# Causal masking of the score maxima: added on TensorE, or inside VectorE's maximum

## The chip, the core and the metric

The kernel runs on one core of one Trainium2 chip. The metric is device time in microseconds (us) from start to end of one launch. Engines are called as in the profile: PE is TensorE's matmul stream and PEld its weight loads, DVE is VectorE, ACT is ScalarE, POOL is GpSimd, SP issues DMAs.

## The reference

Input `x` is 4 batches of 1024 tokens of 256 channels. First, x becomes x + layernorm(g * s), where s is a tanh recurrence over the 1024 tokens of the layer-normed input and g a sigmoid gate. Then x becomes x + layernorm(block(layernorm(x))), where the block is causal attention followed by a top-2-of-4 mixture of experts. The attention, which is what the change touches:

```python
q = _rms(heads(wq), qn_w); k = _rms(heads(wk), kn_w); v = heads(wv)   # 16 heads of 16
scores = jnp.einsum('bhqd,bhkd->bhqk', q, k) * HD ** (-0.5)
scores = jnp.where(causal[None, None], scores, -jnp.inf)
attn = jax.nn.softmax(scores, axis=-1)
```

## The kernel before

The 1024 tokens are cut into 8 chunks of 128 (`NI`); a tile of the attention is one chunk of queries of one batch, 32 tiles in all. For each chunk there are projections for the recurrence, the recurrence itself (one POOL add at L554 and one ACT tanh at L557 per token), layer norms, and projections to q, k, v. A tile of chunk i meets the i+1 key chunks up to its own, for 16 heads: four head groups `hc`, each with four heads on partitions 0, 32, 64 and 96. A block is one pair (hc, key chunk): 128 queries by 128 keys for each of its four heads.

Scores are made twice. "s" has queries on partitions and serves only to find each query's maximum over its keys; the negated maximum is then written into a spare slot of the query vector (`pad[:, 0, :, HD]`), the query is transposed again (`q2`), and "sT" (keys on partitions) comes out of the product with the maximum already taken off. ACT takes the exponential of sT (L979), POOL sets its non-causal entries to zero (L999), and the products with the values are summed in `av` (L1016). A maximum that is too large is harmless for the result of a softmax, as it only rescales numerator and sum.

The blocks of a tile are cut into steps of at most four blocks (`cuts`; chunk 6 alternates four and three). One step for one pair of heads fills two PSUM banks, one per head, up to 512 columns each. `scores()` interleaves the sT products of an earlier tile with the s products of a later one, so that a turn of it takes four of the seven `bank` tiles. Where a step holds a block on the diagonal (key chunk equal to query chunk), the s part ends at L898: a bf16 product of the identity (`ident_h`) with `mask` (0 on and below the diagonal, -3e38 above) adds the mask onto the diagonal blocks of each bank. `look_maxima()` then has DVE reduce each bank with a negated maximum (L937), in one instruction for each run of blocks of one head group, or one for a bank that holds two or four equal runs.

A helper, `Plan`, decides the order in which instructions of all engines are written, from costs given with each `Op` and from which bank or slot would be free first; on the chip each engine runs its own list in that order and waits on semaphores. [...] Banks go back to the plan after the exponential (sT) or after the maximum (s). After the attention come the experts (L1435 to L1574), gathered by token lists.

Of the kernel before, what the change touches and what calls it, by code (L numbers as in the profile page):

```python
# [11 lines left out]
BF16 = mybir.dt.bfloat16  # L12
AF = mybir.ActivationFunctionType
ALU = mybir.AluOpType
# [4 lines left out]
P = 128  # L19
# [18 lines left out]
FMAX = 3.4028234663852886e38  # L38
# [207 lines left out]
def sandwich(  # L246
# [7 lines left out]
    nc = tc.nc  # L254
    ctx.enter_context(tc.manual_schedule())
    wp = ctx.enter_context(tc.tile_pool(name="wp", bufs=1))
# [6 lines left out]
    banks = Banks([psum.tile([P, 512], F32, name=f"bank{n}") for n in range(7)])  # L263
# [30 lines left out]


    ident_h = wp.tile([P, P], BF16, name="ident_h")
    mask = wp.tile([P, P], BF16, name="mask")

    low = wp.tile([P, E, E], F32, name="low")
    nlow = wp.tile([P, E, E], F32, name="nlow")  # L300
# [19 lines left out]
    def once():  # L320

        yield Op("SP", 2.0, 50.0, [ev("x", 0)], lag=8.0)
        for t, ap in loads:
            nc.sync.dma_start(t, ap)
        done("loaded")
        yield Op("DVE", 2.0, 50.0, [ev("st", 0)])
        nc.vector.tensor_copy(ident_h, ident)
        nc.vector.memset(av, 0.0)
        nc.vector.memset(qn_s, 1.0)
        for s in range(4):  # L330
            sl = slice(32 * s, 32 * s + HD)
            nc.vector.tensor_scalar_mul(qn_s[sl], qn_w[sl], HD ** -0.5)

        nc.vector.memset(listed, 0.0)

        nothing = sqs.tiles[0].rearrange("p h d -> p (h d)")[:, :C]
        nc.vector.memset(nothing, 0.0)
        some = nothing.unsqueeze(1)
        for c0, c1 in ((0, C), (2 * C, ROW)):
            nc.sync.dma_start(  # L340
                of_chunk(NI - 1, c0, c1), some[:, :, : c1 - c0].to_broadcast([P, B, c1 - c0])
            )
        for k in range(11):
            nc.sync.dma_start(
                row_d[TOKENS : TOKENS + 1, k * ROW // 11 : (k + 1) * ROW // 11],
                nothing[0:1, : ROW // 11],
            )
        for p in pads.tiles:
            yield Op("DVE", 1.2, 50.0)


            nc.vector.memset(p, 0.0)
            nc.vector.memset(p[:, 1, :, HD : HD + 1], 1.0)
        for cc in range(NCC):
            yield Op("DVE", 1.1, 50.0, [ev("loaded")])
            nc.vector.tensor_scalar_mul(wqk[:, cc, :], wqk[:, cc, :], n1_w[:, cc : cc + 1])
            nc.vector.tensor_scalar_mul(wv[:, cc, :], wv[:, cc, :], n1_w[:, cc : cc + 1])
            nc.vector.tensor_scalar_mul(wg[:, cc, :], wg[:, cc, :], n2_w[:, cc : cc + 1])
        for h in range(0, H, 4):
            yield Op("DVE", 1.2, 50.0)  # L360
            for b in range(B):
                nc.vector.memset(v_all[:, b, :, h : h + 4, HD : HD + 1], 1.0)
        nc.vector.memset(low, 0.0)
        nc.vector.memset(nlow, 1.0)
        for e in range(1, E):
            nc.vector.memset(low[:, e, :e], 1.0)
            nc.vector.memset(nlow[:, e, :e], 0.0)
        yield Op("POOL", 1.5, -1.0)
        nc.gpsimd.memset(mask, 0.0)
        nc.gpsimd.affine_select(  # L370
            out=mask, in_=mask, pattern=[[-1, P]],
            compare_op=ALU.is_ge, fill=NEG, base=0, channel_multiplier=1,
        )
        nc.gpsimd.memset(earlier, 1.0)
        nc.gpsimd.affine_select(
            out=earlier, in_=earlier, pattern=[[1, P]],
            compare_op=ALU.is_gt, fill=0.0, base=0, channel_multiplier=-1,
        )
        nc.gpsimd.memset(every, 1.0)
        for k in range(KINDS):  # L380
            nc.gpsimd.memset(first[:, k : k + 1], float(k * TOKENS))
        nc.gpsimd.tensor_copy(base, first)
        nc.gpsimd.iota(
            number, pattern=[[-P, NI], [-T, B]], base=TOKENS, channel_multiplier=-1,
            allow_small_or_imprecise_dtypes=True,
        )
        nc.gpsimd.iota(
            ramp, pattern=[[1, LISTS]], base=0, channel_multiplier=0,
            allow_small_or_imprecise_dtypes=True,
        )  # L390
        done("once")
# [396 lines left out]
    class Step:  # L788


        def __init__(self, n, number):
            self.n, (self.i, self.b) = n, tiles[n]
            parts = cuts(self.i)
            self.blocks = parts[number]
            self.at = n + number / len(parts)
            self.key = (n, number)
            self.first, self.last = number == 0, number == len(parts) - 1
            self.w = len(self.blocks) * P

            on = [m for m, (_, kb) in enumerate(self.blocks) if kb == self.i]  # L800
            self.diagonal = (on[0], on[1] - on[0] if len(on) > 1 else 1, len(on)) if on else None

            self.mixed = bool(on) and on != [len(self.blocks) - 1]


            runs = {}
            for m, (hc, _) in enumerate(self.blocks):
                runs.setdefault(hc, []).append(m)
            parts_of = [[k for k, part in enumerate(parts) if hc in dict(part)] for hc in range(NHC)]

            def even(part):
                lengths = {sum(h == hc for h, _ in part) for hc in dict(part)}
                return len(lengths) == 1 and len(dict(part)) > 1


            second = lambda hc: max(parts_of[hc], key=lambda k: (even(parts[k]), k))
            self.two = any(len(k) > 1 for k in parts_of)
            self.lone = any(len(k) == 1 for k in parts_of)
            half = lambda hc: int(len(parts_of[hc]) > 1 and number == second(hc))
            if even(self.blocks):  # L820
                self.runs = [(0, len(self.blocks), min(runs), max(runs) + 1, half(min(runs)))]
                assert len({half(hc) for hc in runs}) == 1
            else:
                self.runs = [(r[0], r[-1] + 1, hc, hc + 1, half(hc)) for hc, r in runs.items()]

    tiles = [(i, b) for i in range(NI) for b in range(B)]
    steps = [Step(n, number) for n, (i, b) in enumerate(tiles) for number in range(len(cuts(i)))]
# [2 lines left out]
    def scores():  # L830
# [13 lines left out]
        def block(kind, step, p, pbs, m):  # L844

            hc, kb = step.blocks[m]
            of = q2_of if kind == "sT" else q1_of
            qT = (q2s if kind == "sT" else q1s).tiles[of[step.i, step.b][1]]

            apart = kind == "sT" or not step.mixed  # L850
            for j in range(2):
                sl = slice(32 * (2 * p + j), 32 * (2 * p + j) + 32)
                k = kT[sl, step.b, hc, kb * P : (kb + 1) * P]
                q = qT[sl, hc, :]
                nc.tensor.matmul(  # L855
                    banks.tiles[pbs[j]][:, m * P : (m + 1) * P],
                    lhsT=k if kind == "sT" else q, rhs=q if kind == "sT" else k,
                    start=(m == 0 or apart), stop=(apart and (kind == "sT" or kb < step.i)),
                )

        while na < len(mine) or nl < len(next_):
            todo = []
# [12 lines left out]
            if len(todo) == 1:  # L875
# [2 lines left out]
            longest = max(len(step.blocks) for _, step, _ in todo)  # L878
            masked = sum(
                0.05 + 0.07 * step.diagonal[2]  # L880
                for kind, step, _ in todo if kind == "s" and step.diagonal
            )
            reads = [
                ev("q2" if kind == "sT" else "q1", step.i, step.b) for kind, step, _ in todo
# [8 lines left out]
                    if m < len(step.blocks):  # L893
                        block(kind, step, p, pbs[2 * n : 2 * n + 2], m)
            for n, (kind, step, p) in enumerate(todo):
                if kind == "s" and step.diagonal:
                    for pb in pbs[2 * n : 2 * n + 2]:
                        nc.tensor.matmul(  # L898
                            on_diagonal(banks.tiles[pb][:, : step.w], step), lhsT=ident_h,
                            rhs=mask.unsqueeze(1).to_broadcast([P, step.diagonal[2], P]),  # L900
                            start=False, stop=True,
                        )
                of_step[kind, step.key, p] = pbs[2 * n : 2 * n + 2]
                done(kind, step.key, p)
                if kind == "sT":
                    na += 1
                    if na == len(mine) or mine[na][0].n != step.n:
                        give(q2_of[step.i, step.b])
                else:
                    nl += 1  # L910
                    if nl == len(next_) or next_[nl][0].n != step.n:
                        give(q1_of[step.i, step.b])
# [6 lines left out]
    def look_maxima():  # L919

        for step in steps:
            i, b = step.i, step.b
# [6 lines left out]
            for p in (1, 0):  # L929
                for j in range(2):  # L930
                    for m0, m1, h0, h1, half in step.runs:
# [2 lines left out]
                            [ev("s", step.key, p)],  # L934
                        )
                        pb = of_step["s", step.key, p][j]
                        nc.vector.tensor_reduce(  # L937
                            by_slot[:, half, h0:h1, 2 * p + j],
                            banks.tiles[pb][:, m0 * P : m1 * P].rearrange(
# [747 lines left out]
```

## Time and profile before

| | |
|---|---|
| median of 3 runs | 1494.54 us (1489.77 to 1496.53) |
| the profiled execution's own time | 1487.5 us |
| its span in the profile | 1485.7 us |
| PE, DVE, ACT, POOL busy | 1327.7, 873.2, 723.9, 467.5 us |
| attention and recurrence | to about 1060 us |
| experts | from there to the end |

In the groups of the profile, a line has the engine, the operation, output <- input by name, the shape, the count, then busy time and mean duration of one, then the idle time of the engine just before them and who ended it. The waits list, by pair, who waited for whom: total us, times, longest.

### The profile page before, as it was taken

To read this page: it belongs to the slowest core of one execution; us is meant where nothing else is said; L and a number is where in the kernel's file an instruction comes from. 1 tells how busy PE (TensorE), PEld (TensorE's weight loads), DVE (VectorE), ACT (ScalarE), POOL (GpSimd) and SP (SyncE) were. 2 spreads that over 40 slices of the span, in tenths; PEclk is the share of its full clock that TensorE was granted. 3 is DMA by queue.
4 is the path that set the end of the run, shared out by engine and by line. 5 is a ranking of instruction groups with operands and counts; after the bars stand their busy time and mean duration, and the time that the engine had idled before them with its cause. 6 is when DMAs were issued, how large, how long until landed. Compare 5 with 4: busy or idle time off the path is not lost. (4 is left out here: it accounts for less than half of the span.)

```text
span 1485.7 us, 43429 instructions
## 1 busy us (share of the span) xinstructions
PE 1327.7 (89%) x17800; PEld 1055.8 (71%) x17800; DVE 873.2 (59%) x2419; ACT 723.9 (49%) x2176; POOL 467.5 (31%) x1465
## 2 busy tenths in 40 slices
PE   4568668989999999899999999999999999999994
PEld 2225536656777777777787678878788889888883
DVE  5566668678687588668768776775414312113331
ACT  2345545756756766776654455556422222223220
POOL 2433534535444444344211100101143321214321
PEclk8778878999999999999999999999999999999997
DMA  3010010001010000000001000222031110102200
GB/s 126 29 43 1 15 44 2 16 16 30 3 30 17 2 31 17 3 31 17 3 3 32 17 3 3 56 84 75 16 108 58 51 59 26 40 23 76 56 28 23
DMA packets 35207, 48.73 MB, mean 33 GB/s; under 512 B 7574, under 2 KB 27286, under 8 KB 34966
## 3 DMA queue, kind: packets, MB, share of 16 engines
q1 hardware_dynamic: 28134, 24.94, 5.5%
q0 software_dynamic: 6560, 20.09, 4.7%
q8 instruction: 147, 2.41, 0.7%
q14 instruction: 94, 0.77, 0.2%
q10 hardware_dynamic: 272, 0.52, 0.1%
HBM read 32.34 MB, written 13.73 MB: 31 GB/s over the span
## 5 line engine op out<-in xcount | busy, mean ns | idle before, releaser
L937 DVE TENSOR_REDUCE nm<-bank 128x1 f32<-128x512 f32 (+4 forms) x656 | 373.3, 618 | 144.2 <-PE bank L898 103.4
L979 ACT ACTIVATE ex<-bank 128x512 f32<-128x512 f32 (+1 forms) x592 | 325.7, 581 | 159.3 <-PE bank L855 102.2
L855 PE MATMUL bank<-keys,q 32*128 32x128 f32 x4608 | 346.8, 290 | 14.4 <-ACT ex L979 5.0
L554 POOL TENSOR_TENSOR s<-keys 128x8 f32<-128x8 f32 x1023 | 224.8, 220 | 374.5 <-ACT keys L557 364.1
L855 PE MATMUL bank<-q,keys 32*128 32x128 f32 x4608 | 333.2, 292 | 3.7 <-ACT ex L979 2.4
L557 ACT ACTIVATE keys<-s 128x8 f32<-128x8 f32 x1023 | 218.3, 213 | 206.8 <-POOL s L554 204.5
L855 PEld LDWEIGHTS bank<-q,keys 32*128 32x128 f32 x4608 | 267.9, 190 | 67.9 <-issue 29.6
L855 PEld LDWEIGHTS bank<-keys,q 32*128 32x128 f32 x4608 | 285.0, 190 | 39.0 <-DVE nm L937 13.9
L999 POOL TENSOR_SCALAR_AFFINE_SELECT ex<-ex 128x256 f32<-128x256 f32 (+1 forms) x240 | 103.2, 431 | 290.2 <-ACT ex L979 286.2
L1016 PE MATMUL av<-ex,values 128*17 128x128 f32 x4608 | 162.5, 282 | 2.6 <-DVE avT L1035 2.0
L1456 PE MATMUL bank<-values,keys 128*128 128x256 f32 x632 | 149.5, 383 | 4.7 <-PEq L1620 3.3
L1016 PEld LDWEIGHTS av<-ex,values 128*17 128x17 f32 x4608 | 117.3, 100 | 27.9 <-issue 10.0
L1456 PEld LDWEIGHTS bank<-values,keys 128*128 128x128 f32 x632 | 118.5, 191 | 21.5 <-issue 4.7
L1516 ACT ACTIVATE keys<-bank 128x256 f32<-128x256 f32 x136 | 52.2, 384 | 156.1 <-PE bank L1456 156.0
L1456 PE MATMUL bank<-keys 128*128 128x256 f32 x384 | 84.8, 379 | 0.0
L764 PE MATMUL bank<-ident,pad 128*128 128x128 f32 x384 | 61.5, 293 | 25.8 <-DVE pad L715 23.0
L1456 PEld LDWEIGHTS bank<-keys 128*128 128x128 f32 x384 | 73.0, 190 | 9.9
L505 PE MATMUL bank<-big,wsg 128*128 128x512 f32 x128 | 71.8, 710 | 9.0 <-ACT big L443 5.9
L764 PEld LDWEIGHTS bank<-ident,pad 128*128 128x128 f32 x384 | 45.4, 149 | 36.1 <-ACT keys L557 19.1
L1543 DVE SCALAR_TENSOR_TENSOR rwnext<-av,rwnext 128x192 f32<-128x192 f32 x28 | 10.4, 413 | 101.6 <-PE av L1475 101.6
L1516 ACT ACTIVATE hid<-bank 128x256 f32<-128x256 f32 x66 | 25.4, 384 | 89.5 <-PE bank L1456 89.5
L1475 PE MATMUL av<-keys 128*128 128x192 f32 x384 | 66.4, 326 | 0.0
(232 smaller groups left out, 1687.6 us busy)
## 6 DMA issues: line engine op xcount, KB each, us to landing
row_d<-xn SPq DMA_DIRECT2D x16, 512.0 KB
xn<-in_x SPq DMA_DIRECT2D x8, 512.0 KB
xc<-in_x SPq DMA_DIRECT2D x7, 512.0 KB
keys<-in_e_l SPq DMA_DIRECT2D x2, 1024.0 KB
keys<-in_e_w SPq DMA_DIRECT2D x2, 512.0 KB
keys<-in_e_down SPq DMA_DIRECT2D x2, 384.0 KB
rwnext<-row_d,ids POOLq DMA_INDIRECT x36, 3.8
xc<-in_x SPq DMA_DIRECT2D x4, 128.0 KB
```

The costliest lines, as they stand in the source:

```text
L505: nc.tensor.matmul(pb, lhsT=wsg[:, cc, half * C + dc * P : half * C + (dc + 1) * P], rhs=lnT[:, cc, :], start=(cc == 0), stop=(cc == NCC - 1),
L554: nc.gpsimd.tensor_tensor(s, st[:, :, t], prev, ALU.add)
L557: nc.scalar.activation(st[:, :, t], s, AF.Tanh)
L764: nc.tensor.transpose(banks.tiles[pb][:, hc * P : (hc + 1) * P], flat[:, side, hc * P : (hc + 1) * P], ident,)
L855: nc.tensor.matmul(banks.tiles[pbs[j]][:, m * P : (m + 1) * P], lhsT=k if kind == "sT" else q, rhs=q if kind == "sT" else k, start=(m == 0 ...
L937: nc.vector.tensor_reduce(by_slot[:, half, h0:h1, 2 * p + j], banks.tiles[pb][:, m0 * P : m1 * P].rearrange("p (h w) -> p h w", h=h1 - h0) ...
L979: nc.scalar.activation(exs.tiles[ex[1]][:, j, : step.w], banks.tiles[pb][:, : step.w], AF.Exp)
L999: nc.gpsimd.affine_select(out=d, in_=d, pattern=pattern, compare_op=ALU.is_ge, fill=0.0, base=0, channel_multiplier=-1,)
L1016: nc.tensor.matmul(av[32 * j : 32 * j + HD + 1, hc, :], lhsT=v_all[:, b, kb, 4 * hc + j, :], rhs=exs.tiles[ex[j // 2][1]][:, j % 2, m * P ...
L1456: nc.tensor.matmul(hb[0].tiles[hb[1]], lhsT=w[:, j, m * P : (m + 1) * P], rhs=src[:, j, :], start=(j == 0), stop=(j == nk - 1),)
L1475: nc.tensor.matmul(ob[0].tiles[ob[1]][:, t, :], lhsT=src[:, j, t * P : (t + 1) * P], rhs=w[:, j, :], start=(j == 0), stop=(j == nk - 1),)
L1516: nc.scalar.activation(to, src, AF.Gelu)
```

## The change

Most mask products are taken out. A step is now marked `added` when its diagonal blocks stay with the mask product: all steps of chunks 0 and 1, and the middle step of chunk 2. In the other steps with a diagonal block, a run that ends in its diagonal block is reduced with `tensor_tensor_reduce`: it adds to the run, in place in PSUM, the last columns of a [128, 512] bf16 tile `late` (three blocks of zeros, then the mask), negates, and accumulates the minimum. A run in whose middle the diagonal block lies (one bank with two head groups: the third step of chunk 4, the second and fifth of chunk 5) is reduced as before, with nothing masked.

In the built program each `tensor_tensor_reduce` is two instructions on DVE: the pass over the run, and one that writes the accumulated [128, 1] value. The mask products fall from 416 to 64, and 320 of the 656 maxima take the new form: 176 of 512 columns, 112 of 384, 32 of 128. The costs that `Plan` is given change only for the mask products, and the written order of all engines shifts from chunk 1 on.

```diff
-    mask = wp.tile([P, P], BF16, name="mask")
+    late = wp.tile([P, 4 * P], BF16, name="late")
+    mask = late[:, 3 * P :]
...
+        nc.gpsimd.memset(late[:, : 3 * P], 0.0)
...
-            self.mixed = bool(on) and on != [len(self.blocks) - 1]
...
+            self.added = bool(on) and len(on) == len(self.blocks) // (self.i + 1) and even(self.blocks)
+            self.mixed = self.added and on != [len(self.blocks) - 1]
...
-                    start=(m == 0 or apart), stop=(apart and (kind == "sT" or kb < step.i)),
+                    start=(m == 0 or apart),
+                    stop=(apart and (kind == "sT" or kb < step.i or not step.added)),
...
-                for kind, step, _ in todo if kind == "s" and step.diagonal
+                for kind, step, _ in todo if kind == "s" and step.added
...
-                if kind == "s" and step.diagonal:
+                if kind == "s" and step.added:
...
+                        if not step.added and step.blocks[m1 - 1][1] == i:
+                            w = (m1 - m0) * P
+                            s_ = banks.tiles[pb][:, m0 * P : m1 * P]
+                            nc.vector.tensor_tensor_reduce(
+                                out=s_, in0=s_,
+                                in1=late[:, 4 * P - w :], scale=-1.0, scalar=FMAX,
+                                op0=ALU.add, op1=ALU.min,
+                                accum_out=by_slot[:, half, h0:h1, 2 * p + j],
+                            )
+                            continue
                         nc.vector.tensor_reduce(
```

## Prediction

> **What bounds the kernel now.** I read the busy shares first, then the busy time by stage of the attention, then the rows of the operations that the change touches, then the waits, and last the timeline around single mask products.
>
> ```profile
> PE 1327.7 (89%) x17800; PEld 1055.8 (71%) x17800; DVE 873.2 (59%) x2419; ACT 723.9 (49%) x2176; POOL 467.5 (31%) x1465
> ```
>
> Busy time in six stretches, one per attention chunk from 2 to 7 (length, then PE, PEld, DVE, ACT, POOL with instruction counts, then granted clock, DMA share, GB/s):
>
> ```profile
> 325.00:424.00 99.00, 92.59 (x1502) 70.50 (x1500) 78.77 (x222) 65.21 (x227) 47.03 (x178) 0.98 0.08 24
> 424.00:535.00 111.00, 104.53 (x1829) 81.15 (x1830) 81.90 (x217) 72.93 (x248) 47.17 (x186) 0.92 0.05 12
> 535.00:653.00 118.00, 111.58 (x2152) 87.91 (x2149) 88.60 (x233) 80.66 (x271) 50.35 (x193) 0.96 0.05 16
> 653.00:781.00 128.00, 123.97 (x2556) 97.93 (x2557) 98.20 (x235) 80.89 (x229) 39.14 (x136) 0.99 0.05 15
> 781.00:931.00 150.00, 143.87 (x2950) 112.71 (x2949) 111.47 (x262) 78.75 (x164) 17.77 (x39) 0.99 0.05 13
> 931.00:1060.00 129.00, 125.50 (x2922) 103.79 (x2923) 80.18 (x184) 76.81 (x153) 17.54 (x38) 1.00 0.22 66
> sum 735.00, PE 702.05 PEld 553.98 DVE 539.11 ACT 455.27 POOL 218.99; mean PE 117.01 PEld 92.33 DVE 89.85 ACT 75.88 POOL 36.50
> ```
>
> PE is busy 702 of these 735 us and leaves 33; DVE is next with 539 (73%). All that the change removes lies in these stretches, and all that it adds but one memset. So PE sets the pace, and an instruction taken out of PE's list is worth its time unless another engine comes late. What DVE is late with shows in the waits (total us, times, longest):
>
> ```profile
> PE bank L855 <- DVE nm L937: 3.0, 8, 0.7
> ...
> PEld bank L855 <- DVE nm L937: 25.4, 77, 0.9
> ...
> DVE nm L937 <- PE bank L898: 86.9, 92, 5.2
> ```
>
> Score products stand behind a maximum 85 times, 28.4 us; with L434 (5.2 us) and smaller places about 36 us. In the other direction DVE sits idle 87 us until a mask product is done. The two are coupled by the banks.
>
> **What a removed mask product is worth.** The timeline around two pairs of them (start, duration):
>
> ```profile
> 902.30 0.11 PEld L898 LDWEIGHTS <-ident_h 128*128 128x128 bf16 x2
> 902.31 0.28 PE L898 MATMUL bank<-mask,ident_h 128*128 128x128 bf16 x2
> 902.52 0.79 PEld L1016 LDWEIGHTS av<-ex,values 128*17 128x17 f32 x32
> ...
> 904.62 0.11 PEld L898 LDWEIGHTS <-ident_h 128*128 128x128 bf16 x2
> 904.62 0.29 PE L898 MATMUL bank<-mask,ident_h 128*128 128x128 bf16 x2
> 904.69 0.21 PEld L1060 LDWEIGHTS bank<-ident,row 128*128 128x128 f32 x2
> ```
>
> The busy row (352 products of 229 ns) counts pipelined ends; the path pays start to start. A pair delays the next work by 0.22 us where that is in tiles of the array (32 rows of L855, 17 columns of L1016), as at 902.30, and by 0.07 where it is a full 128x128 product, as at 904.62. Without masks, the step from the last score product to what follows takes 0.20 us, as it does to a mask, so nothing of it is given back. Counted through PE's list after 325 us: 160 groups, 144 of two and 16 of four products, make 352, as many as go (416 less 64). 81 are followed by tiled work, 79 by full: 81 x 0.218 + 79 x 0.072 = 23.4 us; the groups of four cost 0.11 more each, 1.8. **PE: -25.2 us.** The Trainium skill (TensorEngine Tiling, Key Properties) says that a change of tiling mode drains the engine. By that rule alone each removed group would save a drain at both ends, some 160 x 2 x 0.146 = 47 us by the difference of the two rows; the trace shows the drain at one end only, for score products to the next full product take the same 0.20 us with and without a mask, so I stay with the rows.
>
> **What a new maximum costs.** The rows (durations min/median/max in the second to fourth, mean in the first):
>
> ```profile
> L937 DVE TENSOR_REDUCE nm<-bank 128x1 f32<-128x512 f32 x352 | 224.9, 683 | 86.7 <-PE bank L898 47.3 <-PE bank L855 36.8 <-ACT keys L557 1.9
> ...
> L710 DVE TENSOR_TENSOR pad<-pad,rq128y 128x512 f32<-128x512 f32 x20 | 14.2, 709 | 0.2
> ...
> L1093 ACT ACTIVATION_READ_ACCUMULATOR row<-xn x32: 186/188/222, 158.1 to 1057.7; 128x1 f32 x32
> ```
>
> The pass over 512 columns with two inputs is nearest to L710: 709 against 683, +26 ns. The trace has no DVE instruction that reads and writes PSUM, and none that writes out an accumulator. For that second instruction the nearest rows are DVE's small ones: a memset of 16 elements (L715) has a row of 72 ns, two ops of 4 elements without a wait start 77 ns apart (L407 to L409), with a wait on each other 195 (L409 to L410); ACT's own readout has a row of 188. Bounds: +40 ns for pass and readout together (readout nearly hidden: small memsets, L363 to L367, start 9 to 24 ns apart) to +220 (26 + 195). I take 115: 26 plus some 90, nearest to the unwaited pair. The Trainium skill (VectorE: DVE Perf Modes, Two Vector instructions with no wait between them) calls an op with an accumulator output two instructions, as the built list has it, and gives no duration for the second.
>
> **DVE: 320 x 0.115 = +37 us** (13 to 70), 539 to 576 of 735, 78%. Some 64 maxima share a bank with a run that was just written in place (chunks 2 and 4) and now wait for their own engine, 195 less 77 ns each: 7.5 us, within these bounds. Behind them on DVE's list stand the other maxima, copies of `av` and the norms, and behind these PE's next banks.
>
> **What comes late instead.** Each pair of new maxima can start earlier: the second mask product ended 0.198 + 0.036 + 0.229 = 0.46 us after the last score product began, a score product ends 0.27 after, so 0.19 is gained and 2 x 0.115 = 0.23 lost: +0.04 per pair. About a quarter of the maxima hold up PE (85 waits over 328 pairs): 160 x 0.04 x 0.26 = 1.7 us. More weight has the queue: with DVE at 78% and not 73%, I scale the 36 us of waits behind maxima by busy over idle, 3.55 against 2.70: +11 us, an estimate from these rows. ACT stays at 62% and its waits hardly move. The masks that go without any successor (chunk 4's third step, chunk 5's second and fifth, 48 products) cost nothing; the start/stop flags are free. The new memset of 384 bf16 columns on POOL stands at 51 us in the recurrence; the one of 128 took 206 ns, so at most 0.6 us once. The SP list holds the same 65 waits and DMAs with four output and input rows exchanged, far from any bound.
>
> Sum: -25.2 + 1.7 + 11 + 0.6 = **-12 us**; 1487.5 becomes 1475.5 in the profiled execution. That execution lay 7 us below the median of the runs shown, so the median becomes 1494.5 - 12 = 1482.5. The experts' part only starts earlier.
>
> Ends: with readout and pass at 40 ns, 75% and 1.11 x 36: +4, and pairs 0.11 earlier: -5, so -26: 1468. With 220 ns, DVE at 83%: 1.81 x 36 gives +29, pairs 0.25 later +10, so +14: 1509.
>
> **Rivals.**
>
> *DVE streams at half rate.* The new pass reads and writes one PSUM bank; no row shows that. If it takes two cycles per element, 320 passes cost another (176 x 512 + 112 x 384 + 32 x 128) / 0.96 = 143 us (a reduce takes 1.04 ns per column: 683 against 549 for 128 columns less). DVE would hold 539 + 37 + 143 = 719 of 735 us and become the bound: by stretch, chunk 3 alone gets 64 x 0.65 = 41 us, to 123 in 111. At the 95% that PE reaches today, chunks 2 and 3 grow by 5 and 18, the others stay: +17 to +25, 1512 to 1520. For it: nothing shows the opposite. Against: L710 reads two tensors and writes one at full rate, and PSUM reads of 512 columns run at the same rate as SBUF's. It decides from about 0.35 us extra per maximum on. The Trainium skill (Vector Engine (DVE) Microarchitecture Reference, Points that are easy to get wrong) speaks of halved throughput for an op with two non-bf16 SBUF sources; `late` is bf16 and the other source PSUM, so that rule leaves the pass at full rate.
>
> *The saving is eaten.* The extra is near the upper bound, or the shifted order of the lists sets PE's other waits (L764 behind `pad`, 6.5 us; score products behind exponentials, 25 us) so much worse that little is left: within 7.5 us of before, 1487 to 1502. For it: PE's idle time has many owners. Against: the score product's next work is nearly always ready (0.20 us in the median).
>
> *Less is removed than the text says.* Excluded in the count: 64 mask products are left in the list, all of chunks 0 and 1 and 16 of chunk 2.
>
> **How the numbers follow.** A measurement of this kernel tells about 0.5%, 7.5 us, from no change. Forecast (DVE hidden, PE shorter): 0.6, own range 1466 to 1490. Saving eaten: 0.2. Half rate or another large DVE cost: 0.17; the rest in still lower times. The forecast's upper end and the second rival lie partly within 0.5%: faster 0.57, same 0.2, slower 0.23. The range reaches from the cheap end, 1468 less 2 for the scatter of runs, to the 220 ns end, 1466 to 1509; the half-rate rival lies above it.
>
> **What would show it.** Right: 64 mask products, DVE's new rows near 0.71 us with a second row below 0.1, PE's sum in the six chunks near 677, DVE near 576, waits of PE behind maxima 40 to 50 us. Wrong: rows above 1 us; DVE above 90% in chunk 3; PE busy lower but its idle time up by as much.

## The result, and the profile after

| | before | changed |
|---|---|---|
| median | 1496.53 us (1489.77 to 1501.41, 9 runs) | 1505.02 us (1501.09 to 1508.36, 9 runs) |
| profiled execution's own time, span, clock | 1487.5, 1485.7 us, 0.943 | 1501.1, 1499.3 us, 0.938 |

The ratio is 1.0055, 95% interval 1.0038 to 1.0071: 8 us slower, where 12 us faster was forecast. The time lies inside the range, on the other side of no change.

Busy times, from the page of the changed kernel:

```profile
PE 1317.7 (88%) x17448; PEld 1049.8 (70%) x17448; DVE 893.7 (60%) x2739; ACT 724.1 (48%) x2176; POOL 466.6 (31%) x1466
```

TensorE is rid of 352 instructions and 10 us of busy time, VectorE has 320 instructions and 20 us more. PE's idle time over the whole span grew from 158.0 to 181.6 us. The same six stretches of the attention (length, then PE, PEld, DVE, ACT, POOL, then granted clock, DMA share, GB/s):

```profile
325.00:424.00 99.00, 88.38 (x1329) 65.60 (x1324) 73.46 (x253) 59.34 (x202) 43.31 (x164) 0.88 0.06 18
424.00:535.00 111.00, 101.97 (x1744) 79.63 (x1745) 81.76 (x262) 73.33 (x251) 47.16 (x182) 0.94 0.07 22
535.00:653.00 118.00, 106.70 (x1955) 82.67 (x1950) 95.70 (x288) 76.14 (x255) 47.06 (x185) 0.93 0.04 11
653.00:781.00 128.00, 121.84 (x2508) 97.62 (x2512) 99.62 (x271) 85.34 (x255) 43.06 (x158) 0.99 0.05 15
...
sum 735.00, PE 683.87 PEld 541.04 DVE 553.77 ACT 451.38 POOL 216.26; mean PE 113.98 PEld 90.17 DVE 92.30 ACT 75.23 POOL 36.04
```

PE is idler and does not take up other work: in the first three stretches fewer products fit than before (1329, 1744 and 1955 against 1502, 1829 and 2152, of which only 58, 64 and 60 were mask products), and the clock of the first fell from 0.98 to 0.88. VectorE is at 75%.

The new maxima by source line (durations ns min/median/max, first and last start, forms) and as a stretch of the timeline:

```profile
L950 DVE CUSTOM_DVE_ANT_0 bank<-bank,late x320: 273/690/734, 308.3 to 1034.9; 128x512 f32<-128x512 f32 x88, 128x384 f32<-128x384 f32 x48, 128x128 f32<-128x128 f32 x24
L950 DVE DVE_READ_ACCUMULATOR2_ANT nm<- x320: 83/141/145, 308.8 to 1035.6; 128x1 f32 x160
```

```profile
989.82 0.70 DVE L950 CUSTOM_DVE_ANT_0 bank<-bank,late 128x512 f32<-128x512 f32 x1
990.43 0.14 DVE L950 DVE_READ_ACCUMULATOR2_ANT nm<- 128x1 f32 x1
990.43 0.73 DVE L950 CUSTOM_DVE_ANT_0 bank<-bank,late 128x512 f32<-128x512 f32 x1
991.08 0.14 DVE L950 DVE_READ_ACCUMULATOR2_ANT nm<- 128x1 f32 x1
```

The 690 ns are the median over all three widths. Of the 176 passes over 512 columns, the 84 that start alone have a median of 699 ns, and the 92 that start together with the readout of the pass ahead (as at 990.43) have 731. The readout takes 141. Its start does not hold the next instruction back, but a pass that starts with it takes 0.65 us to the next start (990.43 to 991.08), where one that starts alone takes 0.61 (989.82 to 990.43).

Before, VectorE's maxima waited 86.9 us for mask products and 36.8 for score products, 123.7 in all (total us, times, longest):

```profile
DVE nm L937 <- PE bank L855: 36.8, 49, 1.8
```

Now they wait 106.0 us for score products, in two rows:

```profile
DVE bank L950 <- PE bank L863: 59.5, 76, 4.8
DVE nm L957 <- PE bank L863: 46.5, 61, 1.9
```

What ends PE's waits (total us, times, longest), first PE's, then PEld's:

```profile
PE bank L769 <- DVE pad L720: 10.7, 6, 3.3
PE bank L863 <- ACT ex L999: 8.6, 20, 0.5
PE bank L863 <- DVE nm L950: 6.5, 16, 0.8
PE bank L863 <- DVE row L619: 5.2, 5, 1.3
...
PE bank L863 <- DVE nm L957: 2.3, 5, 0.9
```

```profile
PEld bank L863 <- ACT ex L999: 17.8, 41, 0.8
PEld bank L863 <- DVE nm L950: 17.1, 44, 1.0
PEld bank L863 <- DVE nm L957: 17.0, 49, 1.1
...
PEld bank L769 <- DVE pad L720: 7.0, 3, 3.0
PEld bank L863 <- DVE row L619: 6.9, 8, 1.5
```

Score products (now L863) wait 6.5 + 17.1 + 2.3 + 17.0 = 42.9 us for maxima, within the 40 to 50 forecast. Such sums count a wait twice when PE and its weight load sit it out together. Counted once, from the trace, score products waited 25.4 us for maxima before and 34.1 now.

What was not forecast are two waits that come from the preparation of the next chunk's q and k, which no edit of the diff touches. Its transposes at L769 (`heads_T`, L764 before) wait for `pad`: 11.5 us counted once, 7.0 before. And score products wait for banks until the layer norm of the preparation (`row`, L619, L614 before) has read them: 6.9 us, 0.7 before.

### The profile page after: what moved, and what is told of

It reads as the page before. It is cut to its first block, busy times and chain, and to the rows that moved or that the text cites. A ratio compares the mean times of both kernels' runs of the same rounds, so it can differ in the third digit from the quotient of the medians.

```text
span 1499.3 us, 43162 instructions
## 1 busy us (share of the span) xinstructions
PE 1317.7 (88%) x17448; PEld 1049.8 (70%) x17448; DVE 893.7 (60%) x2739; ACT 724.1 (48%) x2176; POOL 466.6 (31%) x1466
## 5 line engine op out<-in xcount | busy, mean ns | idle before, releaser
L999 ACT ACTIVATE ex<-bank 128x512 f32<-128x512 f32 (+1 forms) x592 | 325.8, 581 | 171.8 <-PE bank L863 123.7
L863 PE MATMUL bank<-keys,q 32*128 32x128 f32 x4608 | 353.9, 293 | 25.3 <-ACT ex L999 7.4
L863 PE MATMUL bank<-q,keys 32*128 32x128 f32 x4608 | 334.2, 291 | 3.9 <-ACT ex L999 1.4
L863 PEld LDWEIGHTS bank<-keys,q 32*128 32x128 f32 x4608 | 292.6, 193 | 51.0 <-ACT ex L999 12.6
L863 PEld LDWEIGHTS bank<-q,keys 32*128 32x128 f32 x4608 | 270.9, 189 | 65.3 <-issue 29.9
L957 DVE TENSOR_REDUCE nm<-bank 128x1 f32<-128x512 f32 (+4 forms) x336 | 202.0, 640 | 60.0 <-PE bank L863 46.5
L950 DVE CUSTOM_DVE_ANT_0 bank<-bank,late 128x512 f32<-128x512 f32 (+2 forms) x320 | 188.5, 623 | 67.4 <-PE bank L863 63.9
L1036 PE MATMUL av<-ex,values 128*17 128x128 f32 x4608 | 166.9, 285 | 2.9 <-DVE avT L1055 1.4
L769 PE MATMUL bank<-ident,pad 128*128 128x128 f32 x384 | 64.2, 303 | 29.2 <-DVE pad L720 27.9
L769 PEld LDWEIGHTS bank<-ident,pad 128*128 128x128 f32 x384 | 47.3, 154 | 42.8 <-ACT keys L562 13.4
```

The costliest lines, as they stand in the source:

```text
L769: nc.tensor.transpose(banks.tiles[pb][:, hc * P : (hc + 1) * P], flat[:, side, hc * P : (hc + 1) * P], ident,)
L863: nc.tensor.matmul(banks.tiles[pbs[j]][:, m * P : (m + 1) * P], lhsT=k if kind == "sT" else q, rhs=q if kind == "sT" else k, start=(m == 0 ...
L950: nc.vector.tensor_tensor_reduce(out=s_, in0=s_, in1=late[:, 4 * P - w :], scale=-1.0, scalar=FMAX, op0=ALU.add, op1=ALU.min, accum_out=by ...
L957: nc.vector.tensor_reduce(by_slot[:, half, h0:h1, 2 * p + j], banks.tiles[pb][:, m0 * P : m1 * P].rearrange("p (h w) -> p h w", h=h1 - h0) ...
L999: nc.scalar.activation(exs.tiles[ex[1]][:, j, : step.w], banks.tiles[pb][:, : step.w], AF.Exp)
L1036: nc.tensor.matmul(av[32 * j : 32 * j + HD + 1, hc, :], lhsT=v_all[:, b, kb, 4 * hc + j, :], rhs=exs.tiles[ex[j // 2][1]][:, j % 2, m * P ...
```

## Experiments

All ratios are to the kernel before, with 95% intervals. Kernels called "no mask" have plain maxima over unmasked scores; a maximum that is too large only rescales the softmax. "Prices" are the costs given to `Plan`; they change the written order and nothing else. A time taken from a trace is that of one profiled execution per kernel; a mean clock is that of all executions listed for it.

### The change taken apart: products, maxima, order

The diff changes the price of a score turn along with its work. Four kernels hold one fixed and change the other.

old_order_new_max, the changed kernel with the old prices:

```diff
-                for kind, step, _ in todo if kind == "s" and step.added
+                for kind, step, _ in todo if kind == "s" and step.diagonal
```

> The changed kernel's instructions (352 mask products gone, 320 maxima with the mask inside), but the costs given to the plan count the mask products of all diagonal steps, so that every engine's list stands as in the kernel before. Theory 1 (the loss comes from the written order, which shifted when the mask costs left the plan): the 25 us of PE are got back less some 5 for the maxima, 1470 to 1485, faster than before by 0.8 to 1.7%. Theory 2 (the loss comes from the longer maxima that hold up PE through the banks): as the changed kernel, 1500 to 1508. Theory 3 (mask products stood in time in which PE would have waited anyway, so that nothing is won by their removal): within 5 us of the kernel before.

Measured: 0.9960 (0.9942 to 0.9978), less gain than theory 1 had.

new_order_masks, the kernel before with the new prices:

```diff
-                for kind, step, _ in todo if kind == "s" and step.diagonal
+                for kind, step, _ in todo if kind == "s" and step.added
```

> The kernel before, instruction for instruction (416 mask products, 656 plain maxima), with the plan's costs of the changed kernel, so that every engine's list stands as in the changed kernel. Theory 1 (order): slower than before by what the order costs, 25 us of mask products on top of the changed kernel's time, 1515 to 1532. Theory 2 (longer maxima): within 5 us of the kernel before, as the order matters little. Theory 3 (mask products in idle time): about as the changed kernel, 1500 to 1510, if the order costs something, as before if not.

Measured: 1.0086 (1.0068 to 1.0103), less loss than theory 1 had, more than theory 2, inside theory 3. Not one instruction is added or removed here.

no_mask_new_order, the changed kernel with plain maxima, and no_mask_old_order, the same with the old prices:

```diff
-                        if not step.added and step.blocks[m1 - 1][1] == i:
+                        if False:
```

> The changed kernel with a plain maximum in place of each masked one: the maxima from chunk 2 on (but for chunk 2's middle step) are taken over the whole diagonal block, unmasked; lists in the changed kernel's order. What the new maxima cost is its distance to the changed kernel. Theory 1 (order): little, 2 to 8 us less than the changed kernel, 1497 to 1503. Theory 2 (longer maxima): 25 to 33 us less than the changed kernel, 1472 to 1480. Theory 3: as the kernel before less nothing, 1494 to 1500.

> As the run before this one (plain, unmasked maxima from chunk 2 on, 352 mask products gone), with the mask costs of all diagonal steps left in the plan, so that the lists stand as in the kernel before. It is the removal of the mask products alone. Theory 1 (order) and theory 2 (longer maxima) both: 1494 less 20 to 27 us, 1467 to 1477. Theory 3 (mask products in idle time): within 5 us of the kernel before.

Measured: 1.0000 (0.9986 to 1.0014), where theory 3 lay, and 0.9896 (0.9873 to 0.9918), just short of theories 1 and 2. Theory 3 comes near in three, but the last refutes it: the products alone are worth 15.5 us. The order decides the sign, as in theory 1, at smaller sizes than it had. Together, in us as (ratio - 1) x 1494:

| | products and plain maxima | new maxima | no mask, plain maxima |
|---|---|---|---|
| old order | 0 | -6.0 | -15.5 |
| new order | +12.8 | +8.2 | 0.0 |

So taking the products out is worth 15.5 us (12.8 in the new order), the new maxima cost 9.6 (8.2), and the new order costs 12.8, 14.2 and 15.5 by column. The three add up: -15.5 + 9.6 + 14.2 = +8.3. Each is uncertain by some 3 us. In the old order the change is a gain of 6 us: the order turned the sign.

### Which part of the order

early_costs drops the price only in chunks 2 and 3, late_costs only in chunks 4 to 7:

```diff
-                for kind, step, _ in todo if kind == "s" and step.added
+                ... and step.diagonal and (step.added or step.i >= 4)   # early_costs
+                ... and step.diagonal and (step.added or step.i < 4)    # late_costs
```

> The changed kernel's instructions; the plan leaves out the removed mask products of chunks 2 and 3 alone and still counts those of chunks 4 to 7. Lists as in the changed kernel through chunk 3. The order has been found to cost 12 to 19 us. If it is lost in chunks 2 and 3 and their passage to chunk 4: about the changed kernel, 1.003 to 1.007 of the kernel before. If it is lost later: 0.995 to 0.998, as with the old order.

> The changed kernel's instructions; the plan counts the mask products of chunks 2 and 3 as before and leaves out those of chunks 4 to 7. Lists as in the kernel before through most of chunk 3. If the loss lies in chunks 2 and 3: 0.994 to 0.998 of the kernel before, as with the old order. If it lies in the later chunks: 1.003 to 1.007.

Measured: 1.0059 (1.0035 to 1.0083), as expected, and 0.9929 (0.9904 to 0.9954), a little better than expected. The loss comes from the prices of chunks 2 and 3. There the lists differ most in one place: how many score products stand in PE's list ahead of the first transposes of chunk 4's preparation (`before()`, L594 before, L599 after). It is 944 of 4608 (each product has two rows in the trace) in every old order and in late_costs, and 1120 in every new order and in early_costs. PE's timeline, before and then changed:

```profile
437.57 1.75 PE L594 MATMUL bank<-ident,keys 128*128 128x128 f32 x7
```

```profile
466.77 1.09 PE L599 MATMUL bank<-ident,keys 128*128 128x128 f32 x8
```

The recurrence that these transposes read ended at 434.1 before and 441.5 after, so PE went to them 3.5 us later before and 25 us later after: the list had the attention of chunk 3 first. By the start of the last copies of `av` (L1035, then L1055) chunk 3's attention was done at 519.9 (523.6 before), chunk 4's only at 666.0 (648.5).

The order follows from the prices like this. The plan runs engines' clocks in its own time. A turn with a diagonal block is now 0.24 us or more cheaper, so more turns fit before the planned end of the recurrence, and the preparation, which may not start earlier, slips back in PE's list.

padded_no_mask asks whether another price would do as well: no_mask_new_order with a higher price for every turn.

```diff
-                "PE", 0.22 * longest + 0.2 + 2 * masked, ...
+                "PE", 0.22 * longest + (0.44 if todo[-1][1].i >= 2 else 0.2) + 2 * masked, ...
```

> No mask products and plain maxima from chunk 2 on (but for chunk 2's middle step), as in the two runs without masks; every turn of the score products from chunk 2 on is priced 0.24 us higher in the plan, diagonal or not (the trace shows about 1.5 us from start to start for a turn of four blocks that the plan holds at 1.08). If the old mask cost helped because it kept the plan from running ahead of PE: as the run in the old order or better, 0.982 to 0.992 of the kernel before. If orders merely differ by chance: anywhere from 0.985 to 1.003.

Measured: 0.9963 (0.9945 to 0.9981), short of the old order's 0.9896 and of the 0.982 to 0.992 expected, though better than 1.0000. Chunk 4's preparation stands at 960 in it, 16 products behind 944, and TensorE runs longer at half its clock (71 us from 300 to 1060, no_mask_old_order 48).

### Moving chunk 4's preparation alone

prep_early and prep_late take the changed kernel and lower the planned price of a token of chunk 4's recurrence a little, which moves the plan's idea of when the recurrence ends:

```diff
-                    yield Op("POOL", 0.21, -9.0, [last])
+                    yield Op("POOL", 0.21 - 0.005 * (i == 4), -9.0, [last])
...
-                    yield Op("ACT", 0.21, -9.0, [ev("s")])
+                    yield Op("ACT", 0.21 - 0.005 * (i == 4), -9.0, [ev("s")])
```

prep_late has 0.015 in place of 0.005.

> The changed kernel with one price moved: a token of chunk 4's recurrence costs the plan 0.205 us instead of 0.21. In TensorE's list the first transposes of chunk 4's preparation then stand behind 960 of the 4608 score products, where they stand behind 944 in the kernel before and behind 1120 in the changed kernel; everything up to the products just ahead of that, and the places of chunks 5 to 7, stay as in the changed kernel. Theory late preparation (the order loses its 8 us because chunk 4's preparation is written some 30 us too late): its transposes start near 440 us and not 467, and most of the order's 12 to 15 us come back: ratio 0.993 to 1.000. Rival clock (what the order loses is half-clock stretches that fall as they do in any new order, wherever chunk 4's preparation stands): ratio 1.002 to 1.009, as the changed kernel.

> The control to the kernel with the earlier preparation: the same price moved the same way by 0.015 us instead of 0.005. The order changes as much, but the transposes of chunk 4's preparation stay late, behind 1088 score products. Theory late preparation: as the changed kernel, ratio 1.002 to 1.008, transposes near 460 us. Rival clock: no relation between the two kernels, either may be the faster one.

Measured: 1.0007 (0.9991 to 1.0024) and 1.0031 (1.0017 to 1.0045). The timeline rows of the two, early and late:

```profile
444.98 1.04 PE L599 MATMUL bank<-ident,keys 128*128 128x128 f32 x8
```

```profile
462.63 1.09 PE L599 MATMUL bank<-ident,keys 128*128 128x128 f32 x8
```

The earlier place returns 7 us of the order's 14 (1.0055 less 1.0007), the less late one 3.6. prep_early ended just above, and prep_late inside, the ranges of the theory. Measured side by side, the two differ by 2.7 us in the mean (1.3 to 4.2), and the pair both_early and third_early below, which differs in the same way, by 4.0 (0.9 to 7.1). So the place of chunk 4's preparation is a cause, shown for some 3 to 4 of the order's 14 us. Up to 7 are due to it if all that lies between the changed kernel and prep_early is; that part is not shown, as prep_late, with the preparation only 32 products ahead of the changed kernel's, already returned half of it.

The same price for other chunks tells whether chunk 3's preparation is the other half. Only the chunks and sums differ from the diff above:

| kernel | off the token price | score products ahead of preparations 3, 4, 5 | ratio |
|---|---|---|---|
| both_early | 0.01 in chunks 2 and 3 | 544, 960, 1520 | 1.0002 (0.9985 to 1.0020) |
| third_early | the same, 0.005 in chunk 4 | 544, 1088, 1520 | 1.0029 (1.0009 to 1.0049) |
| both_late | 0.01 in chunk 2, 0.005 in 3 | 656, 1056, 1504 | 1.0078 (1.0052 to 1.0105) |
| both_earlier | 0.01 in chunk 2 | 528, 960, 1504 | 0.9999 (0.9985 to 1.0014) |

> The changed kernel with the plan's price of a token of the recurrence of chunks 2 and 3 at 0.20 us instead of 0.21. In TensorE's list the first transposes of the preparations of chunks 3, 4 and 5 then stand behind 544, 960 and 1520 score products (kernel before: 544, 944, 1504; changed kernel: 560, 1120, 1504; prep_early, ratio 1.0007: 560, 960, 1504). Theory both preparations (chunk 3's being one turn late is the other half of the loss): ratio 0.994 to 0.998. Rival (chunk 3's place does not matter, the other half lies elsewhere): 1.000 to 1.003, as prep_early.

> As both_early, and the tokens of chunk 4's recurrence at 0.205 us in the plan: places 544, 1088, 1520, so chunk 3's preparation early and chunk 4's late. Theory both preparations: between both_early and prep_late (1.0031), 0.998 to 1.002. Rival: 1.002 to 1.005, as prep_late.

> The changed kernel with a token of chunk 2's recurrence at 0.20 us and of chunk 3's at 0.205 us in the plan: places 656, 1056, 1504, so chunk 3's preparation six turns later than in the changed kernel and chunk 4's four turns earlier. Theory both preparations: at least as slow as the changed kernel (1.0055), 1.004 to 1.012. Rival: about prep_late or faster, 1.001 to 1.004.

> The changed kernel with a token of chunk 2's recurrence alone at 0.20 us in the plan: places 528, 960, 1504. Theory both preparations: as both_early or better, 0.993 to 0.998. Rival: 1.000 to 1.003, as prep_early.

The theory of both preparations failed in three of the four: chunk 3's place by one or two turns changes nothing that shows, 1.0002 and 0.9999 equal prep_early, 1.0029 equals prep_late. Only both_late, six turns late, costs what that theory expected. Over the kernels with the new maxima, both_late and the filled ones below apart, the place of chunk 4's preparation sorts the times: 944 gives 0.9929 and 0.9960, 960 gives 0.9999 to 1.0007, 1088 gives 1.0029 and 1.0031, 1120 gives 1.0055 and 1.0059. The kernels without masks go the same way: 944 gives 0.9896 (and 0.9901 and 0.9907 in the last section), 960 gives 0.9963, 1120 gives 1.0000. But 960 is only one turn behind 944: the 6 to 12 us between these two groups are not shown to come from the place.

### What is left: the clock?

With chunk 4's preparation at 960, some 6 us remain against the same work in the old order. One candidate is the clock that TensorE is granted, which the trace records as full or half. In the changed kernel PE's gap ahead of chunk 3's key transposes is followed by half clock:

```profile
403.47 0.63 PE L769 MATMUL bank<-ident,pad 128*128 128x128 f32 x4 [3.27 <-DVE pad L720]
```

```profile
400.00:412.00 12.00, 8.58 (x151) 6.27 (x150) 6.95 (x22) 6.49 (x19) 4.25 (x16) 0.86 0.00 1
```

Added up from the trace's record of the clock, from 300 to 1060 us, the kernel before runs 41 us at half clock, new_order_masks 58, old_order_new_max 48, the changed kernel 65. Half of a difference is lost time, if PE is busy in it (the transposes shown above took 1.75 us for seven at half clock, at 437.57, and 1.09 for eight at full, at 466.77). Over the whole span, for PE's busy time alone (us, one execution each; the clock is the mean of all executions):

| kernel | PE busy | of it at half clock | PE idle | mean clock |
|---|---|---|---|---|
| before | 1327.7 | 108.5 | 158.0 | 0.941 |
| new_order_masks | 1338.0 | 123.3 | 161.4 | 0.938 |
| old_order_new_max | 1306.5 | 110.6 | 173.7 | 0.939 |
| changed | 1317.7 | 129.6 | 181.6 | 0.934 |
| no_mask_old_order | 1296.8 | 106.3 | 172.9 | 0.942 |
| no_mask_new_order | 1311.5 | 139.7 | 176.8 | 0.932 |
| prep_early | 1316.1 | 128.7 | 177.1 | 0.935 |
| both_earlier | 1313.9 | 120.6 | 172.5 | 0.938 |

With the same instructions, the new order keeps PE busy 10.3, 11.2 and 14.7 us longer, and its busy time at half clock is 14.8, 19.0 and 33.4 us longer. Half of that, 7.4, 9.5 and 16.7 us, is lost: in these executions about half of what the order costs (spans 13.7, 19.1 and 18.7 us longer) or more. Idle time grows by 3.4, 7.9 and 3.9. Moving chunk 4's preparation (prep_early against changed) takes 4.5 us of idle time off and leaves the half clock. What is left of the order's loss with the preparation at 960 is in these executions mostly half clock: against old_order_new_max 18.1 us more of it in prep_early (9 us lost) and 10.0 in both_earlier (5 us lost). Why PE is granted less in the new order is another question.

filled_gaps puts products of no use into these gaps, in the changed kernel:

```diff
-            pb, = yield from heads_T(prio + b, pad, 1, [ev("pad", i, b)])
+            pb, = yield from heads_T(
+                prio + b, pad, 1, [ev("pad", i, b)], fill=12 if b == 0 and 3 <= i <= 5 else 0
+            )
...
+        for _ in range(fill):
+            nc.tensor.matmul(banks.tiles[pb], lhsT=ident_h, rhs=late, start=True, stop=True)
```

> The changed kernel with 12 products of 128x512 bf16 (some 2.6 us in all at full clock, their result unused) ahead of the first key transposes of chunks 3, 4 and 5, where PE stands idle 2.3 to 3.2 us for the scaled keys and the granted clock is halved for 3.4 us or more right after. If the halved clock after such gaps is part of the loss: the half-clock stretches at about 404, 517 and 619 us are gone, 3 to 6 us less than the changed kernel, 0.999 to 1.003 of the kernel before. If the clock does not follow the gaps: the stretches stay and the time is the changed kernel's or up to 4 us more.

Measured: 1.0022 (1.0003 to 1.0041), inside the range for the clock. In the stretch shown above the clock is restored:

```profile
400.00:412.00 12.00, 11.19 (x177) 7.61 (x176) 8.36 (x25) 7.39 (x23) 4.76 (x19) 1.00 0.01 1
```

But half clock came elsewhere: the sum is 65 us as without the filling, and the mean clock of all executions is 0.935, as against 0.934. So at most 2 to 3 of the 5 us gained (the intervals just overlap) can be put down to the clock. Gaps like these are not the whole reason either: of the changed kernel's 13 stretches of half clock from 300 to 1060 us only four have a gap of PE of over 2 us in the 7 us ahead of them. prep_early_filled and both_earlier_filled have the same filling in the better orders:

> prep_early (1.0007) with 12 idle-time products of 128x512 bf16 ahead of the first key transposes of chunks 3, 4 and 5, as in filled_gaps; their result is overwritten. Instructions otherwise in the same order. prep_early has 65 us at half clock from 300 to 1060 us, the kernel before 41. Theory clock (what is left of the order's loss is half-clock time after waits of TensorE for `pad`): half-clock time falls below 55 us and the ratio to 0.995 to 0.999. Rival (the rest has nothing to do with the clock, or the stretches only move): 1.000 to 1.004.

> both_earlier (0.9999) with the same 12 products in the same three places; both_earlier has 58 us at half clock from 300 to 1060 us and waits 21 us for `pad` at the transposes. Theory clock: below 50 us, ratio 0.994 to 0.998. Rival: 0.999 to 1.003.

Measured: 1.0012 (0.9997 to 1.0026) with 68 us at half clock, and 0.9986 (0.9974 to 0.9998) with 48. The first gained nothing, although its mean clock rose from 0.935 to 0.938. The second has as little half clock as old_order_new_max from 300 to 1060 us and is still some 4 us slower (the intervals just overlap), though its 36 extra products take time too (8.3 us of rows in filled_gaps). So the filling took the half clock away in single places and did not show what causes it. The table shows that the remaining loss goes along with half clock; what brings that about in the new order stays open.

### Does a better version exist

no_mask_late_costs is late_costs with plain maxima; no_mask_anywhere also drops the 64 products of chunks 0 to 2 (`self.added = False`) and keeps the prices of before.

> The kernel late_costs (the mask price dropped for chunks 4 to 7 alone) with plain, unmasked maxima in place of the new ones; the non-causal scores of these steps then count in the maximum, which only makes it larger. Its list has chunk 4's preparation behind 944 score products. Theory: order good (late_costs had 0.993) and 8 to 12 us less for the maxima: ratio 0.985 to 0.989, as no_mask_old_order (0.990). Rival: the new maxima cost nothing here, ratio 0.993.

> No mask product at all, those of chunks 0 and 1 and of chunk 2's middle step too, every maximum a plain reduce over unmasked scores, the prices and so the order of the kernel before. Against no_mask_old_order (0.990) 64 more products go, 32 groups of two: by that kernel's own 18.7 us for 160 groups about 3.7 us more, ratio 0.985 to 0.989. Rival: chunks 0 to 2 wait for the recurrence and not for TensorE, so these products cost nothing: ratio 0.989 to 0.992.

Measured: 0.9907 (0.9883 to 0.9931) and 0.9901 (0.9879 to 0.9923). Neither beats no_mask_old_order, 0.9896. The second lies where the rival had it, but what the 64 products of chunks 0 to 2 cost is not shown: its mean clock is 0.934 (no_mask_old_order 0.942), and its PE is busy 136.1 us at half clock where that kernel's is 106.3, which is 15 us lost and may hide what was won. Against late_costs (0.9929) the maxima are worth 3 us, in overlapping intervals: between the two expectations, and less than the 9.6 of the table. The fastest of these versions is to mask nothing ahead of the maxima and keep the old prices: 15 us below the kernel before.

## Why the prediction was wrong

**The written order: the step that failed.** The prediction counted the shift of the lists at nothing and named it only in the rival "the saving is eaten", at 0.2. It measured +12.8 us with not an instruction changed (new_order_masks) and +14.2 under the new maxima. The order was there to be read before any run: 176 more score products stood ahead of chunk 4's preparation. I compared what was removed and added, and not where the other work had gone. In the profiled executions the order's cost is about half or more PE at half clock, and otherwise mostly idle time. Chunk 4's place is shown to account for some 3 to 4 us of it; why the clock is lower in the new order stays open. The prediction's own sign of being wrong came true: PE's busy time fell by 10.0 us while its idle time rose by 23.6.

**The products: -25.2 forecast, -15.5 measured.** The work did leave PE: in no_mask_old_order its busy time, pipelined ends included, falls by 30.9 us, 1327.7 to 1296.8. The forecast was even too small by its own method. It read the delay ahead of full products, 0.072 us, from the next weight load (904.62 to 904.69); from product to product, the step across a pair of mask products is 0.325 us and without them 0.200, so 0.125, and the sum becomes -29.3. But about half came back: PE's idle time rose from 158.0 to 172.9 us. The sentence that ACT's waits hardly move was wrong. From the waits of no_mask_old_order, PE and then PEld:

```profile
PE bank L863 <- ACT ex L999: 12.0, 21, 1.6
PE bank L863 <- DVE nm L957: 5.4, 10, 1.1
```

```profile
PEld bank L863 <- DVE nm L957: 26.8, 72, 1.3
PEld bank L863 <- ACT ex L999: 23.8, 52, 1.8
```

Counted once, score products wait 23.9 us for banks that exponentials hold, 17.8 before, and 26.8 for maxima, 25.4 before. The rest of the idle time is spread over smaller waits.

**The new maxima: +12.7 forecast, +9.6 measured.** The sum came out by luck; its parts did not hold. Back to back and from start to start, a pass of 512 columns takes 608 ns against 598 for a plain reduce, one of 384 takes 473 against 465 and one of 128 takes 206 against 198: some 9 ns more, where 26 was taken. The readout has 141 ns, above the forecast of 90, but it adds less: 42 ns to a pass that starts with it (132 times), and 175 ns where another maximum waits for it (55 times). Together 320 x 0.009 + 132 x 0.042 + 55 x 0.175 = 18.0 us, where 37 was taken, inside the bounds of 13 to 70; busy time rose by 20.5. The queue term, 11 us, scaled 36 us of waits that hold some twice (the 8 waits in PE's row lie inside the 77 of PEld's) by a busy share of 78%. In old_order_new_max it is 76%, for which the same scaling gives 6. Counted once, the waits of score products for maxima rose from 25.4 to 33.7, by 8.3. So too large a cost of the maxima met too weak a scaling.

**The rival of half rate** is out: a pass over 512 columns that starts alone takes 699 ns, in place and with two inputs, against 683 for the plain reduce (this agrees with the page cited there). The memset of `late` took 412 ns, once. The count of 64 products held.

## What to carry to other kernels

Where a planner writes the order from prices, a change of prices is an edit of its own: rebuild the kernel with only the new prices, compare the lists of the engine that sets the pace, and look for the work that feeds the next stage having slipped behind more of this one. Measure work and order apart, as a 2 x 3 table does here, before believing that an instruction was costly, and set the time at half clock beside each time. Of the time taken from the engine with most work, expect part back as idle time: here 14.9 of 30.9 us.

## What the runs showed of the hardware

VectorE's readout of an accumulator has a row of 141 ns, and the next instruction starts in the same 0.01 us (990.43) unless it waits for VectorE itself; then it starts 175 ns after the readout (72 times in the changed kernel). The readout is not free for a pass of the same kind that starts with it: that takes 649 ns from start to start and not 608. An in-place pass over a PSUM bank with a second operand in SBUF, back to back with another instruction's work and without a readout, takes 608 ns per 512 columns, 2% more than a reduce that only reads (598).

The clock went to half after gaps of PE that are short: 3.27 us ahead of 403.47. The Trainium skill (TensorE: Matmul & The Clock Gate, Part 1: The HAM clock gate) has the throttle return after an idle window of about 3.4 us. The gap seen here lies a little below that, and half clock also came without one: in the 7 us ahead of the stretch that begins at 421.07 PE's longest gap was 0.30 us.
